# Leaky ReLUs of a graph-attention layer: from VectorE instructions to ScalarE's Prelu

## The chip, the cores and the metric

The kernel runs on one core of one Trainium2 chip. The metric is device time in microseconds (us), here of that one core. Engines are named as the profile names them: PE is TensorE's matmul, PEld its weight load, DVE is VectorE, ACT is ScalarE, POOL is GpSimd, SP is SyncE, whose queue issues nearly all transfers. Each engine works through its own queue in order and waits on semaphores for the others.

## The reference, cut to what matters

There are 128 graphs of 128 nodes with 512 features. Layer 0 is masked multi-head attention with 8 heads, a ReLU, a residual and a layer norm. Layer 1, in which the change lies, is graph attention with one head:

```python
Wh = jnp.matmul(h, W)                      # h is layer 0's output
s_i, s_j = Wh_sg @ a1, Wh_sg @ a2
e = _leaky(s_i[:, :, None] + s_j[:, None, :])      # first leaky ReLU, slope 0.2
e = jnp.where(adj > 0, e, jnp.float32(-9000000000000000.0))
attention = jax.nn.softmax(e, axis=1)
h_prime = jnp.einsum('bij,bjf->bif', attention, Wh)
return _leaky(h_prime)                             # second leaky ReLU
# outside: x = _layernorm(x + layer1(x))
```

So for each of the 128 graphs a leaky ReLU is applied to a 128x128 matrix ahead of the softmax, and another one to the 128x512 product behind it.

## The kernel before, in words

All data is float32. The kernel goes over the graphs in two interleaved streams. The projections of layer 0 (`st_` banks, matmuls of L367) are made for groups of four graphs, the output projection of layer 0 and the projection of layer 1 (banks `p_y`, `p_w`, `p_x`, matmuls of L448) for pairs; each of these products is a seven-product block scheme whose partial results ScalarE copies out of PSUM (L344, L348, L459, L770) and VectorE adds up. Attention of layer 0 is the class `Softmax` (logits L520, exponentials L554, division L568, product L600), its norm is `LayerZero`, and layer 1's projection is `LayerOne`.

The class `Edge` is layer 1 behind its projection, one object for each graph. Its methods, in order:

- `sender` (L798, ScalarE) adds s_i to the mask; the result is transposed, for 117 graphs by a store (L806), a fetch (L812) and a block transposition on VectorE (`turn_blocks`, L817), for the last 11 by TensorE into the PSUM bank `p_e` (`turn`, L802).
- `add` (L820, ScalarE) adds s_j, a value for each partition, to the transposed matrix.
- `maxima` (VectorE) applies the leaky ReLU into the tile `att` (L825) and takes the row maxima of that, negated (L827).
- `exp` (L831, ScalarE) exponentiates and sums; `divide` (VectorE) takes the reciprocal (L835) and scales (L836).
- `product` (L841, TensorE) multiplies by `Wh` into the bank `p_h`.
- `copy` (L847, ScalarE) copies that bank into the tile `z`.
- `residual` (VectorE) applies the second leaky ReLU in place (L851) and adds the residual (L852).
- `stats` (L644 and L646, VectorE), `rstd` (L650 and L652, POOL), `apply` (L665 on VectorE or L661 on ScalarE) and `store` (SP queue, L865) are the layer norm and the output.

The order of all instructions is written out by hand. A loop over steps `t` covers the first 124 graphs, in pairs of steps with one order for even and one for odd `t`; in both `edge.add()` comes directly ahead of the block that holds `edge.maxima()` and `fin.residual()`, where `fin` is the edge one step older. The last graphs are ordered by a string, `PLAN`, which names a job and a method for each piece; `e0` to `e10` are the last eleven edges. In the loop the tile `att` has two buffers and `z` one; in the plan these tiles lie in the space of weights that are no longer needed, which the profile calls `wk` and `wq`.

Two more names occur below: `wv_n` (L408) is a ring of weight blocks fetched from DRAM for the value projection, and `x_dram` (L716) is the store of layer 0's output, fetched back transposed as `xz` (L241).

Of the kernel before, what the change touches and what calls it, by code (L numbers as in the profile page):

```python
# [11 lines left out]
AF = mybir.ActivationFunctionType  # L12
ALU = mybir.AluOpType
# [6 lines left out]
ALPHA = 0.2  # L20
# [4 lines left out]
def kernel(  # L25
# [59 lines left out]
    nc = tc.nc  # L85
    B, P, D = x.shape
# [9 lines left out]
    small = ctx.enter_context(tc.tile_pool(name="small", bufs=3))  # L96
# [136 lines left out]
    X, XT, XS, Q, K, V, MF, OT, X1T, X1, WH = ({} for _ in range(11))  # L233
# [59 lines left out]
    )  # L293

    def strassen(bank, multiply, read, add):


# [17 lines left out]
        def block(h, o, role, name=None):  # L315
            return lambda: add(h, o, p[role], t.get(name))

        return {
            "p1": product("y", 0, True),
            "t0": copy("t0", 0),  # L320
            "p5": product("w", 4, True),
            "p6": product("y", 5),
            "t2": copy("t2", 1),
            "p2": product("x", 1, True),
            "c11": block(0, 0, "x", "t0"),
            "p7": product("y", 6),
            "t3": copy("t3", 1),
            "c22": block(1, 1, "w", "t3"),
            "p4": product("y", 3),
# [20 lines left out]
    def group_product(g, turn, weight, out, transposed_out, bias=None):  # L350
# [30 lines left out]
        def add(h, o, p, t):  # L381
            if t is None:
                copy_out(out(h, o), p, o, bias)
            else:
                nc.vector.tensor_add(out(h, o), p, t)

        return strassen(bank, multiply, read, add)

    def products(g):
# [110 lines left out]
    class Softmax:  # L500
# [28 lines left out]
        def add(self, r):  # L529
            if r == 0:  # L530
                self.pa = self.tile("pa", [P, 4, H, 32])
            by_head = self.pa.rearrange("p b h k -> p h b k")
            mf = MF[self.b].rearrange("p (b k) -> p b k", b=4)
            nc.vector.tensor_add(  # L534
                by_head[:, r * NC : (r + 1) * NC],
                self.lg[r].rearrange("p c (b k) -> p c b k", b=4),
                mf.unsqueeze(1).to_broadcast([P, NC, 4, 32]),
            )
# [8 lines left out]
        def maxima(self):  # L547
            self.add(0)
            self.add(1)
            self.reduce()  # L550
# [58 lines left out]
        def copy(self):  # L609
            pair, h = divmod(self.b, 2)  # L610
            if h == 0:
                OT[pair] = self.tile("oT", [P, NC, 2 * P])
            for c in range(NC):
                nc.scalar.activation(  # L614
                    OT[pair][:, c, h * P : (h + 1) * P],
                    self.oT[:, c, :],
                    AF.Identity,
                    bias=b_cols[:, 1, c : c + 1],
                )
# [49 lines left out]
    class LayerZero:  # L669
# [12 lines left out]
        def residual(self, h, src, o=None):  # L682
            dst = X1[2 * self.pair + h]
            if o is not None:
                dst = dst[:, o * HALF : (o + 1) * HALF]
            nc.vector.scalar_tensor_tensor(dst, src, 0.0, dst, op0=ALU.max, op1=ALU.add)
# [94 lines left out]
    class Edge:  # L781
# [35 lines left out]
            nc.vector.transpose(self.e, self.ez.rearrange("p a e -> p (a e)"))  # L817

        def add(self):
            nc.scalar.activation(self.e, self.p, AF.Identity, bias=self.s[:, 1, :])  # L820

        def maxima(self):
            e = self.e
            self.att = self.tile("att", [P, P], small, 2)
            nc.vector.scalar_tensor_tensor(self.att, e, ALPHA, e, op0=ALU.mult, op1=ALU.max)  # L825
            self.nmax = small.tile([P, 1], F32, name="nmax1", bufs=4)
            nc.vector.tensor_reduce(self.nmax, self.att, AX.X, ALU.max, negate=True)  # L827

# [15 lines left out]

        def copy(self):
            self.z = self.tile("z", [P, D], work, 1)
            nc.scalar.copy(self.z, self.ph)  # L847

        def residual(self):
            z = self.z  # L850
            nc.vector.scalar_tensor_tensor(z, z, ALPHA, z, op0=ALU.mult, op1=ALU.max)  # L851
            nc.vector.tensor_add(z, z, X1.pop(self.b))  # L852

        def stats(self):
            self.norm = Norm(self.z, self.on_scalar)
# [567 lines left out]
```

## Time and profile before

| | |
|---|---|
| three timed runs, us | 2368.99, 2369.56, 2372.61 |
| median, us | 2369.56 |
| span of the profiled execution, us | 2364.5 |
| own device time of the profiled execution | not recorded beside the span; the median of the timed runs is 5.1 us above it |
| granted TensorE clock, mean | 0.998 |
| busy: PE, PEld, DVE, ACT, POOL, us | 2330.4, 1976.3, 1836.7, 1507.4, 769.9 |
| instructions in the span | 43985 |

The span is the time from the first to the last instruction in one profiled execution. A share of busy time is an average over the whole span: the profile has a short start-up, a long even stretch in which the same two steps come again and again, and a drain of some 110 us at the end, and these have to be looked at one by one. A matmul counts as busy from its start to a modelled end, so neighbouring matmuls overlap. An idle gap is shown with the instruction whose end is taken to have released the engine.

### The profile page before, as it was taken

How to read it: one execution, taken by the hardware profiler on the slowest of the kernel's cores; microseconds unless marked ns; L12 is line 12 of the kernel's file. 1: busy time of each engine (PE TensorE's matmuls, PEld its weight loads, DVE VectorE, ACT ScalarE, POOL GpSimd, SP SyncE). 2: the span in 40 equal slices, each digit the busy share in tenths (PEclk: the TensorE clock that was granted, in tenths of full speed). 3: DMA queues.
4: the chain of work that ended last, by engine and by line, in shares of the span. 5: the costliest groups of instructions: out<-in, count | busy, mean ns of one | idle time of the engine just before them, and what ended most of it. 6: DMA issues, size and time to landing. Idle time of an engine off the chain costs nothing.

```text
span 2364.5 us, 43985 instructions
## 1 busy us (share of the span) xinstructions
PE 2330.4 (99%) x13362; PEld 1976.3 (84%) x13362; DVE 1836.7 (78%) x3718; ACT 1507.4 (64%) x5459; POOL 769.9 (33%) x1191
## 2 busy tenths in 40 slices
PE   8999999999999999999999999999999999999997
PEld 7878888888888888888888888888888888888875
DVE  5677787877878877878778778778787787787778
ACT  3656666667666666666576666666665766666675
POOL 2232333323333323333233333233332333332325
PEclk9999999999999999999999999999999999999999
DMA  6655555555555555555555555555555555555453
GB/s 196 189 158 164 169 165 178 163 164 169 173 158 175 166 168 165 168 170 173 163 171 167 163 175 168 168 163 170 172 169 164 170 168 163 176 167 168 152 164 114
DMA packets 435564, 395.31 MB, mean 167 GB/s; under 512 B 108280, under 2 KB 339328, under 8 KB 435328
## 3 DMA queue, kind: packets, MB, share of 16 engines
q1 hardware_dynamic: 435008, 392.23, 54.2%
q8 instruction: 107, 1.75, 0.3%
q14 instruction: 129, 1.06, 0.2%
q10 hardware_dynamic: 320, 0.26, 0.0%
HBM read 248.58 MB, written 143.72 MB: 166 GB/s over the span
## 4 chain that ended last, share of the span: by engine, by line
PE 85%; DVE 5%; DMA 4%; ACT 3%; issue 1%; SPq 1%; POOL 1%; DVEq 0%; POOLq 0%; ACTq 0%
PE st_y L367 25%; PE p_y L448 16%; PE st_w L367 13%; PE p_w L448 8%; PE st_x L367 6%; PE lg L520 5%; PE p_oT L600 4%; PE p_h L841 4%; PE p_x L448 4%; ACT pa L568 1%; DMA paz<-pa_dram 1%; DMA pa_dram<-pa 1%; DVE st L644 1%; DVE pa L534 1%; DVE nmax L543 0%
## 5 line engine op out<-in xcount | busy, mean ns | idle before, releaser
L650 POOL TENSOR_SCALAR ve<-mv 128x1 f32<-128x1 f32 x256 | 69.8, 273 | 1425.4 <-DVE mv L646 1420.0
L554 ACT ACTIVATE pa<-pa,nmax 128x128 f32<-128x128 f32 x1008 | 393.4, 394 | 5.6 <-DVE nmax L543 5.5
L568 ACT ACTIVATE pa<-pa,rs 128x128 f32<-128x128 f32 x1008 | 326.6, 391 | 28.5 <-DVE rs L564 28.5
L344 ACT COPY st_t<-st_y 128x512 f32<-128x512 f32 x192 | 111.0, 578 | 158.9 <-PE st_y L367 83.2
L459 ACT COPY pr_t<-p_y 128x257 f32<-128x257 f32 (+1 forms) x375 | 137.3, 366 | 110.8 <-PE p_y L448 109.9
L348 ACT ACTIVATE st_t<-st_y,b_cols 128x256 f32<-128x256 f32 x192 | 79.9, 467 | 198.9 <-PE st_y L367 198.9
L554 ACT ACTIVATION_READ_ACCUMULATOR pa<-pa,nmax 128x1 f32 x1008 | 192.3, 191 | 0.0
L587 DVE STREAM_TRANSPOSE pa<-paz 128x1024 f32<-128x1024 f32 x126 | 156.9, 1245 | 18.1 <-DMA paz<-pa_dram 15.6
L534 DVE TENSOR_TENSOR pa<-lg,mf 128x512 f32<-128x512 f32 x252 | 161.0, 680 | 0.2 <-PE lg L520 0.2
L614 ACT ACTIVATE oT<-p_oT,b_cols 128x128 f32<-128x128 f32 x504 | 137.1, 381 | 33.8 <-PE p_oT L600 33.6
L543 DVE TENSOR_REDUCE nmax<-pa 128x8 f32<-128x1024 f32 x126 | 151.7, 1204 | 2.2
L652 POOL TENSOR_TENSOR rstd<-ve,mhalf 128x1 f32<-128x1 f32 x256 | 146.2, 571 | 21.3
L600 PEld LDWEIGHTS p_oT<-pa,v 128*64 128x64 f32 x2016 | 108.6, 137 | 49.5 <-issue 23.7
L520 PE MATMUL lg<-kT,qT 64*128 64x128 f32 x2048 | 132.1, 279 | 0.0
L448 PE MATMUL p_y<-wo,oT 128*128 128x256 f32 x504 | 129.6, 380 | 1.7 <-ACT p_y L469 1.7
L448 PE MATMUL p_y<-w,x1T 128*128 128x257 f32 x496 | 128.8, 382 | 1.7 <-ACT wk L459 1.6
L448 PE MATMUL p_y<-wo,oS 128*128 128x256 f32 x504 | 129.5, 379 | 0.5 <-ACT pr_t L459 0.5
L520 PEld LDWEIGHTS lg<-kT,qT 64*128 64x128 f32 x2048 | 119.4, 188 | 12.3 <-issue 11.6
L448 PE MATMUL p_y<-w,x1S 128*128 128x257 f32 x496 | 128.0, 380 | 0.2 <-ACT wk L459 0.2
L600 PE MATMUL p_oT<-pa,v 128*64 128x128 f32 x2016 | 125.0, 276 | 2.3 <-DVE pa L587 1.9
L367 PE MATMUL st_y<-wv_n,xT 128*128 128x256 f32 x512 | 121.3, 380 | 3.3 <-ACT st_t L344 3.3
L367 PE MATMUL st_y<-xT,wk 128*128 128x256 f32 x512 | 124.0, 385 | 0.0
(201 smaller groups left out, 5869.6 us busy)
## 6 DMA issues: line engine op xcount, KB each, us to landing
pa_dram<-pa SPq DMA_DIRECT2D x126, 512.0 KB, 2.9
paz<-pa_dram SPq DMA_DIRECT2D x504, 128.0 KB, 2.8
wv_n<-wv SPq DMA_DIRECT2D x224, 256.0 KB, 3.0
x<-in_x_dram SPq DMA_DIRECT2D x128, 256.0 KB, 2.9
x_dram<-x SPq DMA_DIRECT2D x128, 256.0 KB, 2.3
xz<-x_dram SPq DMA_DIRECT2D x512, 64.0 KB, 2.0
xz<-in_x_dram SPq DMA_DIRECT2D x496, 64.0 KB, 2.3
out_dram<-z SPq DMA_DIRECT2D x120, 256.0 KB, 2.5
```

Source lines behind the costliest of these rows:

```text
L367: nc.tensor.matmul(p[:, m, :], lhs, rhs, start=start and m == 0 and kc == 0, stop=True, skip_group_check=True,)
L448: nc.tensor.matmul(p[:, :width], xs()[n][:, kc, :], w[:, PLACE[n], kc, :], start=start and kc == 0, stop=True, skip_group_check=True,)
L459: nc.scalar.copy(t[:, :width], p[:, :width])
L520: nc.tensor.matmul(self.lg[r][:, c, :], q[rows, c, cols], k[rows, c, cols], start=c == 0, stop=True, skip_group_check=True,)
L534: nc.vector.tensor_add(by_head[:, r * NC : (r + 1) * NC], self.lg[r].rearrange("p c (b k) -> p c b k", b=4), mf.unsqueeze(1).to_broadcast( ...
L543: nc.vector.tensor_reduce(self.nmax, by_head, AX.XY, ALU.max, negate=True)
L554: nc.scalar.activation(self.pa[:, :, h, :], self.pa[:, :, h, :], AF.Exp, bias=self.nmax[:, h : h + 1], accum_out=self.sums[:, h : h + 1],)
L568: nc.scalar.activation(self.pa[:, :, h, :], self.pa[:, :, h, :], AF.Copy, scale=self.rs[:, h : h + 1])
L587: nc.vector.transpose(self.paT.rearrange("p h (a i) -> p a h i", i=32), self.paz.rearrange("p a (h k) -> p a h k", k=32),)
L600: nc.tensor.matmul(self.oT[r * HD : (r + 1) * HD, c, :], v[:, h * HD : (h + 1) * HD], self.paT[:, r * NC + c, :], start=c == 0, stop=True, ...
L614: nc.scalar.activation(OT[pair][:, c, h * P : (h + 1) * P], self.oT[:, c, :], AF.Identity, bias=b_cols[:, 1, c : c + 1],)
L652: nc.gpsimd.tensor_tensor(self.r, ve, mhalf, ALU.pow)
```

## The change

The two leaky ReLUs move from instructions of their own on VectorE into the two ScalarE instructions that come ahead of them. `add` now computes Prelu(p + s_j) with slope 0.2 and writes straight to `att`; `copy` computes Prelu of the PSUM bank. The tile `att` is taken in `add` instead of `maxima`. Nothing else is moved: the loop, the plan and all other instructions stand where they stood, and lines behind L820 are up to two lower or one higher in the file.

```diff
         def add(self):
-            nc.scalar.activation(self.e, self.p, AF.Identity, bias=self.s[:, 1, :])
+            self.att = self.tile("att", [P, P], small, 2)
+            nc.scalar.activation(
+                self.att, self.p, AF.Prelu, bias=self.s[:, 1, :], alpha=ALPHA
+            )
 
         def maxima(self):
-            e = self.e
-            self.att = self.tile("att", [P, P], small, 2)
-            nc.vector.scalar_tensor_tensor(self.att, e, ALPHA, e, op0=ALU.mult, op1=ALU.max)
             self.nmax = small.tile([P, 1], F32, name="nmax1", bufs=4)
             nc.vector.tensor_reduce(self.nmax, self.att, AX.X, ALU.max, negate=True)
...
         def copy(self):
             self.z = self.tile("z", [P, D], work, 1)
-            nc.scalar.copy(self.z, self.ph)
+            nc.scalar.activation(self.z, self.ph, AF.Prelu, alpha=ALPHA)
 
         def residual(self):
-            z = self.z
-            nc.vector.scalar_tensor_tensor(z, z, ALPHA, z, op0=ALU.mult, op1=ALU.max)
-            nc.vector.tensor_add(z, z, X1.pop(self.b))
+            nc.vector.tensor_add(self.z, self.z, X1.pop(self.b))
```

## The prediction

> **What bounds the kernel now.** I read the page's busy times first, then the busy time by stretch, then what TensorE waited for, then VectorE's timeline at the end. The page says that TensorE is all but full:
>
> ```profile
> PE 2330.4 (99%) x13362; PEld 1976.3 (84%) x13362; DVE 1836.7 (78%) x3718; ACT 1507.4 (64%) x5459; POOL 769.9 (33%) x1191
> ```
>
> The table of stretches (start:end and length in us, then busy us of each engine) shows where the 1% is:
>
> ```profile
> 150.00:400.00 250.00, 247.32 (x1431) 210.42 (x1430) 194.43 (x390) 158.62 (x579) 81.29 (x122) 1.00 0.54 166
> 400.00:1000.00 600.00, 599.51 (x3469) 510.74 (x3468) 473.14 (x954) 384.83 (x1398) 194.26 (x300) 1.00 0.55 168
> ...
> 2255.00:2320.00 65.00, 59.95 (x368) 46.57 (x367) 50.39 (x105) 50.15 (x177) 24.76 (x49) 1.00 0.51 163
> 2320.00:2364.00 44.00, 31.06 (x116) 20.09 (x114) 36.12 (x86) 21.07 (x55) 24.32 (x48) 0.91 0.31 106
> ```
>
> From 400 to 1000 us PE is idle for 0.5 us of 600, and the two stretches up to 2255 us look alike (0.3 us each). There VectorE, busy for 79%, is cover only. PE has gaps from 150 to 400 us (2.7 us) and in the drain: 5.1 us from 2255 to 2320, 12.9 us after. No edge work lies before 148 us, where L825 first runs, so the 11.9 idle us before 150 us stay. The change can win about 21 us at the very most. What PE waited for, first from 150 to 2255 us, then from 2255 us on (total, times, longest):
>
> ```profile
> PE st_y L367 <- ACT st_t L344: 1.9, 1, 1.9
> PE st_w L367 <- DVE x1T L246: 0.5, 2, 0.3
> PE p_oT L600 <- DVE pa L587: 0.4, 1, 0.4
> ```
>
> ```profile
> PE p_h L841 <- DVE wk L836: 4.5, 5, 2.6
> PE p_y L448 <- ACT wk L459: 1.7, 3, 0.9
> PE st_y L367 <- DMA wv_n<-wv: 1.7, 1, 1.7
> ```
>
> The largest is the division L836 ahead of an edge product, and on VectorE the removed instructions stand ahead of that division. The last one, 2.6 us at 2349.6 us, leads into the chain that sets the end.
>
> **What the skill says.** (1) The Trainium skill, "ScalarE: Activation LUTs", section *What ACT_TABLE_LOAD costs*, gives one element per cycle for every function: 186 ns + 0.833 ns an element with immediates, 280 ns + 0.833 with one pointer operand. That is 613 ns for a 128x512 activation with immediates and 387 ns for 128x128 with a pointer bias; the trace has 586 ns for the present copy L847 and 406 for L820, within 5%. (2) "ScalarE activation tables: per-element evaluation and per-set limits", section *What a function is on this engine*: with the same operands an activation costs the same whichever table is read, functions in one set need no switch, and a switch is one load of 1283 ns. The trace has a single load, of 1283 ns, at 2.6 us; no run here shows Prelu yet. In the built program of the changed kernel there is again one load, with Exp and Prelu both behind it. (3) "Trainium Kernel Development and Optimization", section *Performance Expectations*, warns that matmul busy time is a poor measure since matmuls overlap. So I checked the pace: in the chain that ended last, four matmuls of 256 columns take 0.86 or 0.87 us everywhere in the even part. Full there does mean full.
>
> **The change part by part.** The rows concerned (count, then total us and mean ns):
>
> ```profile
> L851 DVE SCALAR_TENSOR_TENSOR z<-z 128x512 f32<-128x512 f32 x120 | 81.2, 677 | 0.1
> ...
> L825 DVE SCALAR_TENSOR_TENSOR att<-e_turned 128x128 f32<-128x128 f32 x117 | 42.3, 361 | 0.2 <-ACT e_turned L820 0.2
> ...
> L847 ACT COPY z<-p_h 128x512 f32<-128x512 f32 x120 | 70.3, 586 | 83.5 <-PE p_h L841 74.0 <-DMA out_dram<-z 4.3 <-DMA paz<-pa_dram 4.0
> ...
> L820 ACT ACTIVATE e_turned<-e_turned,wh 128x128 f32<-128x128 f32 x117 | 47.5, 406 | 6.5 <-DVE e_turned L817 6.5
> ...
> L920 ACT ACT_TABLE_LOAD x1 | 1.3, 1283 | 2.6 <-issue 2.6
> ```
>
> *Removed from VectorE:* 128 instructions of L851 (120 x 677 ns and 8 x 672 ns: 86.6 us) and 128 of L825 (117 x 361 and 11 x 376: 46.4 us), 133 us in all.
>
> *On ScalarE:* no instruction more. `add` keeps its operands, so I take 0 for it. `copy` goes from a copy to an activation with immediates. Bounds: nothing below the copy's 586 ns is to be expected since both read and write the same elements, and above, the skill's 613 (+27 ns), or the nearest activation of that size in the trace, with two pointers, 829 ns (L661; +243 ns). I take +0.02 us; 128 x 0.02 = 2.6 us on ScalarE, at most 31. In the even part ScalarE is busy for 23.4 us of the 36.2 us of a pair of graphs, and waits for PE before these very copies (74.0 us at L847), so either bound is hidden there by PE.
>
> *Waits.* `add` now writes `att`. In the built program it waits in the loop for VectorE's transposition alone, so the two buffers of `att` bring no wait for a product; the copies of `p_y` queued behind it are not held up. L827 waits for ScalarE instead of for L825, and `add` stands well ahead of it. PE, POOL and the SP queue keep their order, and no transfer is added. With orders fixed and hardly any duration longer, things can only come earlier, apart from contention.
>
> *What is gained, 150 to 2255 us.* The 1.9 us gap at 174 us: TensorE waits for st_t on ScalarE, that is queued behind L568, which waits for the reciprocal L564, and in front of this VectorE works without a break from 165.3 us, an L825 (0.3) and an L851 (0.7) among it. Gain 1.0. The 0.4 us at 379 us (L587, behind a fetch whose chain has an L851 and an L825): gain 0.4. What is late elsewhere is PE itself: 133 us of VectorE's work end in idle time. Sum 1.4; bounds 0 and 2.3.
>
> *Drain up to 2349.6 us.* The 1.7 us for wv_n at 2271.5 us follow from a chain of L851 (0.6 at 2261.0), norm, store x_dram, and its fetch in the SP queue ahead of the wv_n fetch: gain 0.7. Four of the five waits for L836 sum to 4.5 - 2.6 = 1.9 us, with an L825 ahead of each and an L851 ahead of most: gain 1.4. The waits for L459 (1.7) are partly behind an exponential that waits for L827: gain 0.4. The wait for rt L835 (0.4): 0.2. What is late next is ScalarE, without a break from 2275.6 to 2286.7 us, and PE. Sum 2.7; bounds 1 and 5.
>
> *The last chain*, from the timeline of VectorE (start, duration):
>
> ```profile
> 2349.41 0.69 DVE L851 SCALAR_TENSOR_TENSOR wq<-wq 128x512 f32<-128x512 f32 x1 [0.70 <-ACT wq L847]
> 2350.14 0.69 DVE L852 TENSOR_TENSOR wq<-wq,x 128x512 f32<-128x512 f32 x1
> 2350.75 0.28 DVE L825 SCALAR_TENSOR_TENSOR wk<-wk 128x128 f32<-128x128 f32 x1
> 2351.07 0.29 DVE L827 TENSOR_REDUCE nmax<-wk 128x1 f32<-128x128 f32 x1
> ...
> 2352.45 0.28 DVE L825 SCALAR_TENSOR_TENSOR wk<-wk 128x128 f32<-128x128 f32 x1
> ...
> 2357.32 0.66 DVE L851 SCALAR_TENSOR_TENSOR wq<-wq 128x512 f32<-128x512 f32 x1
> 2358.01 0.69 DVE L852 TENSOR_TENSOR wq<-wq,x 128x512 f32<-128x512 f32 x1
> 2358.74 0.69 DVE L644 BATCH_NORM_STATS2 st<-wq 128x6 f32<-128x512 f32 x1
> ```
>
> Without L851 the addition starts at 2349.41, the maxima at 2350.14 (`add` on ScalarE ends at 2349.65), instead of 2351.07: -0.93. The second L825, 0.32 with its gap, goes too: the division of the last edge ends 1.25 earlier, and so do its product and its copy, which ended at 2357.07 and would end at 2355.82. From that copy to the end of the statistics were 2.57 us (2359.64); without L851, and with the statistics of the edge before finished by 2355.7, they are 0.03 + 0.73 + 0.89 = 1.65: -0.92. Sum 2.2; 0.06 for longer copies is within rounding; with the upper bound on the copies some 0.5 less.
>
> Total: 1.4 + 2.7 + 2.2 = 6.3 us. The span goes from 2364.5 to 2358.2; with the 5.1 us by which the median stands above the span, 2369.6 goes to **2363.3**.
>
> **The rivals.** (a) *PE takes the gaps back*: another input is late next at each gap, and only the last chain's 2.2 us stay: 2367.4, no change that can be told. For it: the chain that ended last names ScalarE and DMA in the drain as well. Against it: VectorE heads PE's waits there. (b) *Slower: activation tables reload* between Exp and Prelu, on ScalarE, 1283 ns a switch (the row above). Of the eleven last edges each would switch up to four times: 44 x 1.283 = 56 us, where ScalarE is idle for 65 - 50.2 + 44 - 21.1 = 37.8 us from 2255 us on; 18 us over, so 2369.6 - 6.3 + 18 = 2381 and more if the even part (10.3 of 12.8 idle us a pair) breaks too. It decides from some five switches in the last chain, which eat the 6.3 us. Against it: one load in the built program. (c) *Prelu is simply dearer* than a copy. With the upper bound, three on the last path cost 0.7 us: 2364. It would need over 2 us each to lose.
>
> **How the numbers follow.** Told apart from no change is about 0.2%, 4.7 us. The forecast has 0.69: it ranges over the bounds 0 to 2.3, 1 to 5 and 1.5 to 2.5, so 2.5 to 9.8 us, of which I put 0.05 under 4.7 us. Rival (a) has 0.23, (c) counts inside these two, (b) and unseen contention 0.08, of which 0.02 end within 0.2%. Faster 0.64, same 0.30, slower 0.06. The range reaches from 2369.6 - 9.8, and 1 us for the scatter of the runs (3.6 us between the three shown), 2359, to 2368, past rival (a).
>
> **What would show it.** Right: L851 and L825 gone, DVE near 1704 us, ACT within 10 us of 1507, one table load, PE's busy time unchanged, the gap at 174 us near 0.9, PE's waits for L836 nearly halved, and the last statistics some 2 us nearer to the last copy's start. Wrong: more table loads, Prelu rows over 0.7 us, or gaps of the same length with other releasers.

## The result and the profile after

| | before | after |
|---|---|---|
| timed runs, us | 2368.99 to 2372.61 (4) | 2350.80 to 2352.52 (4) |
| median, us | 2369.89 | 2351.74 |
| ratio, 95% interval | | 0.9927 [0.9914, 0.9940] |
| span of the profiled execution, us | 2364.5 | 2350.7 |
| device time of that execution, us | not recorded | 2352.52 |

The change wins 18.1 us, three times the 6.3 forecast, and 2351.7 lies below the range. In the page's line of busy times only VectorE moved by much, by 129.8 us; ScalarE did not:

```profile
PE 2324.7 (99%) x13362; PEld 1978.8 (84%) x13362; DVE 1706.9 (73%) x3462; ACT 1506.7 (64%) x5459; POOL 763.0 (32%) x1191
```

The groups of instructions of the kernel after (count, total us, mean ns, idle time before, and its releasers) show what the new ScalarE instructions cost, 599 and 406 ns, and that there is one table load:

```profile
L847 ACT ACTIVATE z<-p_h 128x512 f32<-128x512 f32 x120 | 71.9, 599 | 78.0 <-PE p_h L841 55.0 <-DMA paz<-pa_dram 22.0 <-DMA out_dram<-z 0.4
...
L821 ACT ACTIVATE att<-e_turned,wh 128x128 f32<-128x128 f32 x117 | 47.5, 406 | 2.5 <-DVE e_turned L817 2.4
...
L918 ACT ACT_TABLE_LOAD x1 | 1.3, 1283 | 2.6 <-issue 2.6
```

The table of stretches of the kernel after (start:end, length, busy us of PE, PEld, DVE, ACT, POOL, then the clock's share). The last two stretches are those of before from 2255 us on, counted back from the end:

```profile
150.00:400.00 250.00, 249.89 (x1445) 213.29 (x1444) 183.31 (x371) 160.62 (x587) 81.88 (x124) 1.00 0.55 168
400.00:1000.00 600.00, 600.00 (x3479) 513.36 (x3478) 441.00 (x890) 386.19 (x1405) 194.99 (x302) 1.00 0.55 168
2241.20:2306.20 65.00, 61.65 (x382) 49.40 (x381) 45.88 (x96) 49.22 (x183) 22.52 (x40) 1.00 0.51 162
2306.20:2350.70 44.50, 34.86 (x139) 24.39 (x137) 34.04 (x82) 25.85 (x62) 26.71 (x62) 0.97 0.38 128
```

From 400 to 1000 us PE's busy time grew by 0.5 us, but there are 10 matmuls more in the same 600 us (3479 against 3469). That is the gain which idle time doesn't show: ten matmuls at a pace of 0.216 us, that of the 256-column ones, are about 2.2 us. In the drain, PE did 382 + 139 = 521 matmuls in its last 109.5 us, where before did 368 + 116 = 484 in 109.

**Where the time came from.** Both traces hold the same 13362 matmuls in the same order. The table gives the time between the same two of them, in us; the columns' heads are the times in the profile of before. The first column counts from the first matmul (1.3 us after the span's start), and the last from the last `p_w` matmul at 2349.6 us, so it has the last wait and the last edge products in it. "Again" and "third" are further profiles of the same two programs (from the experiments).

| | start to 165 | 165 to 400 | to 1000 | to 1600 | to 2241 | to 2320 | to 2350 | to the end |
|---|---|---|---|---|---|---|---|---|
| before | 163.9 | 235.14 | 599.86 | 599.82 | 641.09 | 78.99 | 29.48 | 14.88 |
| before, again | 164.4 | 234.43 | 598.63 | 600.29 | 641.34 | 84.05 | 29.49 | 14.20 |
| before, third | 166.0 | 239.92 | 601.79 | 600.64 | 641.13 | 81.97 | 29.51 | 14.22 |
| after | 166.1 | 231.67 | 597.89 | 598.48 | 639.84 | 77.21 | 26.53 | 11.70 |
| after, again | 163.1 | 233.48 | 597.71 | 598.41 | 639.84 | 80.22 | 26.55 | 11.69 |

(The start is free of the change: it varies mostly in one stretch, 60 to 95 us, ahead of all edge work, that takes 34.1 to 38.4 us over all programs profiled, and 34.1 and 37.9 us in the two profiles of after.) The even part from 165 to 2241 us gives 3.46 + 1.96 + 1.34 + 1.25 = 8.0 us, the drain up to 2349.6 us 1.8 + 2.95 = 4.7, the last chain 3.2, and the start takes 2.2: 13.7 us of span. The rest of the 18.1 lies between the profiled executions and the medians. Around the span are 2352.52 - 2350.7 = 1.8 us (1.7 to 1.9 in nearly every run); with these the profiled execution of before took 2366.3 us, 3.6 below its median, and that of after 0.8 above its own. The profile of before is of a short execution. The profiles "again" are of longer ones (2369.99 and 2354.18 us): there the even part gives 5.2, the drain 6.8, the last chain 2.5 and the start 1.4, 15.9 in all. So the split of the gain by stretches depends on which executions were profiled; the third profile of before has an even part of 2083.5 us, where the other two have 2075.9 and 2074.7.

**The waits.** In the even part of after no idle gap of PE is left to list. The waits of PE's weight loads (total, times, longest) had shown more than PE's own gaps. Before, from 150 to 2255 us, without the rows that both kernels have alike:

```profile
PEld st_w L367 <- DVE x1T L246: 3.3, 6, 0.7
PEld st_y L367 <- ACT st_t L344: 2.3, 1, 2.3
PEld p_y L448 <- ACT pr_t L459: 2.1, 5, 0.6
PEld p_w L448 <- issue: 1.6, 4, 0.5
PEld p_oT L600 <- DVE pa L587: 0.9, 2, 0.7
PEld st_w L367 <- issue: 0.9, 3, 0.3
```

In the two rows with "issue" the profile finds no releaser. The same view of after, from 150 to 2241 us, all that is left beside the common rows:

```profile
PEld st_y L367 <- ACT st_t L344: 0.5, 1, 0.5
PEld p_oT L600 <- DVE pa L587: 0.2, 1, 0.2
PEld st_w L367 <- issue: 0.2, 1, 0.2
```

These six rows of before sum to 11.1 us, 8.6 of them with a releaser named; 0.9 are left after. The Trainium skill, "Perfetto Trace Analysis", section *Identifying the Most-Contended Engine*, says that matmul busy time doesn't tell how near to its limit TensorE is, since its instructions are pipelined, and names the share of peak arithmetic and the busy share of the weight loads as the measures. On busy time the case agrees (the share of the weight loads, 84% before and after, tells little here; their waits do): a matmul of 256 columns is shown for some 380 ns and the next starts 216 ns later, so one that comes up to 160 ns late leaves no gap at all.

One late engine, VectorE, can be followed behind most of these rows. ScalarE's wait for VectorE's reciprocal, in the row of the softmax division, first in before and then in after:

```profile
L568 ACT ACTIVATE pa<-pa,rs 128x128 f32<-128x128 f32 x1008 | 326.6, 391 | 28.5 <-DVE rs L564 28.5
```

```profile
L568 ACT ACTIVATE pa<-pa,rs 128x128 f32<-128x128 f32 x1008 | 327.6, 397 | 0.7 <-DVE rs L564 0.6
```

**How VectorE's lateness gets into a prefetch.** One of the nine places where `st_w` came late, in the timeline of before (start, duration, engine):

```profile
826.86 1.55 DVE L665 TENSOR_SCALAR z<-z,mv,rstd 128x512 f32<-128x512 f32 x1
...
828.43 0.34 SPq L865 DMA_DIRECT2D out_dram<-z  x1
...
828.86 0.39 SPq L806 DMA_DIRECT2D e_dram<-e  x1
...
829.34 0.40 SPq L408 DMA_DIRECT2D wv_n<-wv  x1
...
831.19 1.29 DVE L246 STREAM_TRANSPOSE x1T<-xz 128x512 f32<-128x512 f32 x2
...
832.62 1.75 PE L367 MATMUL st_w<-wv_n,xT 128*128 128x256 f32 x7 [0.30 <-DVE x1T L246]
```

The same place after:

```profile
823.17 1.54 DVE L665 TENSOR_SCALAR z<-z,mv,rstd 128x512 f32<-128x512 f32 x1
...
824.74 0.34 SPq L863 DMA_DIRECT2D out_dram<-z  x1
...
825.17 0.39 SPq L806 DMA_DIRECT2D e_dram<-e  x1
...
825.65 0.41 SPq L408 DMA_DIRECT2D wv_n<-wv  x1
...
828.54 1.29 DVE L246 STREAM_TRANSPOSE x1T<-xz 128x512 f32<-128x512 f32 x2
...
829.73 1.46 PE L367 MATMUL st_w<-wv_n,xT 128*128 128x256 f32 x6
```

The store of `z` waits for the norm L665 on VectorE, and the SP queue works in order, so the fetch of `wv_n` behind the store waits too. It takes 3.1 us to land: in before at 829.34 + 3.14 = 832.48 us, and the matmul starts at 832.62. The profile puts this wait down to the transposition `x1T` of VectorE, which ends at 832.48 too. But the matmul doesn't read `x1T`, and in after it starts at 829.73, while that transposition still runs, to 829.83. After, the norm starts 6.6 us ahead of the matmul instead of 5.8, and the fetch goes out 4.1 us ahead of it instead of 3.3, so it lands about 1 us before it is needed.

In the drain PE's waits of after, from 2241 us on, are these (before: 4.5 for L836, 1.7 for L459 and 1.7 for `wv_n`):

```profile
PE p_h L841 <- DVE wk L836: 1.9, 2, 1.5
PE p_y L448 <- ACT wk L459: 1.3, 2, 0.9
PE st_y L367 <- DMA wv_n<-wv: 1.1, 1, 1.1
```

### The profile page after: what moved, and what is told of

It reads as the page before. It is cut to its first block, busy times and chain, and to the rows that moved or that the text cites. A ratio compares the mean times of both kernels' runs of the same rounds, so it can differ in the third digit from the quotient of the medians.

```text
span 2350.7 us, 43613 instructions
## 1 busy us (share of the span) xinstructions
PE 2324.7 (99%) x13362; PEld 1978.8 (84%) x13362; DVE 1706.9 (73%) x3462; ACT 1506.7 (64%) x5459; POOL 763.0 (32%) x1191
## 4 chain that ended last, share of the span: by engine, by line
PE 92%; DMA 3%; DVE 2%; ACT 1%; SPq 1%; issue 1%; POOL 0%; POOLq 0%; DVEq 0%; ACTq 0%
PE st_y L367 26%; PE p_y L448 18%; PE st_w L367 13%; PE p_w L448 9%; PE st_x L367 7%; PE lg L520 5%; PE p_oT L600 5%; PE p_h L841 4%; PE p_x L448 4%; DMA paz<-pa_dram 1%; DMA pa_dram<-pa 1%; ACT pa L568 0%; ACT pa L554 0%; SPq L581 0%; DMA e_dram<-e 0%
## 5 line engine op out<-in xcount | busy, mean ns | idle before, releaser
L459 ACT COPY pr_t<-p_y 128x257 f32<-128x257 f32 (+1 forms) x375 | 139.0, 371 | 125.1 <-PE p_y L448 120.7
L587 DVE STREAM_TRANSPOSE pa<-paz 128x1024 f32<-128x1024 f32 x126 | 156.9, 1246 | 15.7 <-DMA paz<-pa_dram 14.1
```

The costliest lines, as they stand in the source:

```text
L459: nc.scalar.copy(t[:, :width], p[:, :width])
L587: nc.vector.transpose(self.paT.rearrange("p h (a i) -> p a h i", i=32), self.paz.rearrange("p a (h k) -> p a h k", k=32),)
```

## The experiments

Three accounts of the excess were set against each other. *Occupancy*: VectorE does too much in a pair of steps, and taking 122 us out of the loop lets it run ahead wherever that work stands. *Chain*: only what stands directly ahead of the maxima and the norm matters. *Store*: the work matters since it delays the store of `z` that the fetch of `wv_n` is queued behind. "Even part" is the time from the matmul at 165 us to that at 2241 us, against 2075.9 us in the first profile of before. In the texts of what was expected, theory Q is occupancy and S the store; C puts the waits down to VectorE's and ScalarE's own lateness without the store, and E holds that the even part is covered by TensorE and the gain comes from the last edges. Each group of runs has its own runs of before: median 2372.56, 2373.46 and 2371.18 us.

### The loop alone and the plan alone

`loop_only` makes both edits for the 117 edges of the loop, `plan_only` for the eleven of the plan; VectorE's two instructions are left out for the same edges (not in the cut):

```diff
+            if not self.homes:        # loop_only; plan_only: if self.homes:
+                self.att = self.tile("att", [P, P], small, 2)
+                nc.scalar.activation(
+                    self.att, self.p, AF.Prelu, bias=self.s[:, 1, :], alpha=ALPHA
+                )
+                return
             nc.scalar.activation(self.e, self.p, AF.Identity, bias=self.s[:, 1, :])
...
+            if not self.homes:        # plan_only: if self.homes:
+                nc.scalar.activation(self.z, self.ph, AF.Prelu, alpha=ALPHA)
+            else:
+                nc.scalar.copy(self.z, self.ph)
```

> Both Prelus for the 117 edges of the loop alone; the eleven edges of the plan keep VectorE's leaky ReLUs. Theory Q (VectorE's queue): in the even part the removed instructions had stood ahead of what TensorE waits for, in many waits too short to be shown as idle time; of the 16 us by which TensorE came earlier after 165 us in the changed kernel 8.0 lie before 2241 us, so this kernel should win about 8 us (6 to 11) and its drain should be as long as in the kernel before. Theory E (end chain): the even part is covered by TensorE and the gain comes from the last edges; this kernel should win at most 2 us.

> Both Prelus for the last eleven edges alone. Theory Q: only the drain gains, 4.8 us of waits up to the last products and 3.2 behind them, so 8 us (6 to 10), and the waits in the even part stay as in the kernel before (weight loads of st_w waiting some 3 us in all). Theory E: nearly the whole 18 us.

`loop_only`: 2361.34 us, 0.9956 [0.9938, 0.9973]. Its even part is 8.3 us shorter, stretch by stretch as in after; from 2241 us to the end it gains 0.4. `plan_only`: 2365.70 us, 0.9975 [0.9963, 0.9986]; its even part is 1.2 us longer than before's, and from 2241 us on it gains 1.1, 2.9 and 3.2, as after does. So the two parts are separate and, within intervals of some 3 to 4 us each way, add up: 11.2 + 6.9 = 18.1 us. The weight loads of `plan_only` wait as before in the even part:

```profile
PEld st_w L367 <- DVE x1T L246: 4.4, 9, 0.8
PEld p_oT L600 <- DVE pa L587: 2.7, 6, 0.9
```

### One leaky ReLU each

```diff
 # z_only: L825 stays, L851 goes
-            nc.scalar.copy(self.z, self.ph)
+            nc.scalar.activation(self.z, self.ph, AF.Prelu, alpha=ALPHA)
 # att_only: L851 stays, L825 goes
-            nc.scalar.activation(self.e, self.p, AF.Identity, bias=self.s[:, 1, :])
+            nc.scalar.activation(
+                self.att, self.p, AF.Prelu, bias=self.s[:, 1, :], alpha=ALPHA
+            )
```

> Only the second leaky ReLU (128x512, 677 ns on VectorE) is moved into the copy. Theory Q: gain in proportion to VectorE's removed time, 86.6 of 133 us, so about 12 us of 18 (9 to 14). Theory E: the two on the last chain count 0.73 and 0.92, the rest of the drain about half, so about 5 us.

> Only the first leaky ReLU (128x128, 361 ns) is moved into the addition of s_j. Theory Q: 46.4 of 133 us, so about 6 us of 18 (4 to 9); both parts together should about add up to the whole. Theory E: about 3 us. If instead one part alone wins nearly the whole, a threshold at one wait decides and not the sum of the time.

`z_only`: 2358.12 us, 0.9935 [0.9918, 0.9953], a gain of 14.4. `att_only`: 2361.44 us, 0.9956 [0.9941, 0.9971], a gain of 11.1. They sum to 25.6 where both together give 18.1, and both are above what had been expected of them (9 to 14 and 4 to 9 us in proportion to VectorE's time, 5 and 3 by the end of the kernel alone). In the even part each alone gives most of it, 6.9 and 6.3 us of 8.0. The stretches say why: several kernels end on the same 597.71, 598.41 and 639.84 us from 400 to 2241 us (`att_only` the first two, `z_only` the last two, `loop_only`, `no_leaky` and `after_again` all three). That is taken for TensorE's own time, with nothing waited for: no kernel is below it. To take away 46 us of VectorE's work or 87 us of it leads to this floor in two of three stretches.

### The store behind the fetch

`before_order` is the kernel before with one call moved: the loop issues the store of `z` behind `e_dram` and the fetch of `wv_n` (the call stood once in the order for even and once in that for odd steps; the cut shows one). `after_order` has the same move made in the kernel after.

```diff
                 fin.apply()
-                fin.store()
...
             group()
+            fin.store()
```

> The kernel before, with the loop's store of the result z issued on the SP queue after the fetch of wv_n and the store of e that used to stand behind it; VectorE's work is the one of before. Theory S (SP queue): in the even part most of the lost time comes from wv_n landing late, since its fetch stands behind a store that waits for VectorE's norm; this order alone should win the wv_n part of the ledger, about 3 us of the profile's 8, and more where the runs of before scatter upward. Theory C (compute waits): the waits are for VectorE's additions and for ScalarE's copies behind the reciprocals, so the order changes less than 1 us.

> The changed kernel with the same order of the store. Its even part has no waits left by the profile, so both theories expect no change against the changed kernel (2350 to 2354). If it is faster, waits too short to be seen were still there; if slower, the late store of z holds up the next copy into z.

`before_order`: 2367.15 us, 0.9975 [0.9964, 0.9986]: 6.3 us by the medians (some 3 to 9 with the interval), a third of the gain, with none of VectorE's work taken away. In the profile the even part is 3.5 us shorter, and 3.0 of that are the late starts of `st_w`: all nine are gone, as the store account had said (about 3). Its timeline at the place shown above:

```profile
825.83 1.54 DVE L665 TENSOR_SCALAR z<-z,mv,rstd 128x512 f32<-128x512 f32 x1
...
826.35 0.32 SPq L806 DMA_DIRECT2D e_dram<-e  x1
...
826.76 0.38 SPq L408 DMA_DIRECT2D wv_n<-wv  x1
...
827.39 0.34 SPq L865 DMA_DIRECT2D out_dram<-z  x1
...
831.11 1.89 PE L367 MATMUL st_w<-wv_n,xT 128*128 128x256 f32 x8
```

The fetch goes out before the norm ends and 4.4 us ahead of its matmul. The row `st_w <- DVE x1T` is gone from the waits of weight loads, though the transposition `x1T` is still there: it was not a wait for `x1T`. Of what stays, the largest rows with a releaser are VectorE's work itself and ScalarE's copies:

```profile
PEld p_oT L600 <- DVE pa L587: 1.7, 6, 0.5
PEld st_y L367 <- ACT st_t L344: 1.5, 1, 1.5
```

`after_order`: 2355.50 us, 0.9923 [0.9904, 0.9942], in its bounds the same as after, and its even part is 0.3 us longer. With the VectorE instructions gone, the order of the store brings nothing more.

### VectorE's work put back in another place

`filler_late` is the kernel after with instructions of the removed sizes put back behind the statistics, where no maximum and no residual has their result as an input. They change no value. The norm's application and the store of `z` do stand behind them.

```diff
             self.norm.stats()
+            if not self.homes:
+                for part in (self.z, self.z[:, :P]):
+                    nc.vector.scalar_tensor_tensor(part, part, 1.0, part, op0=ALU.mult, op1=ALU.max)
```

> The changed kernel with two VectorE instructions of the removed kind and sizes put back in each loop edge, without effect on the values, directly behind the statistics: VectorE is as busy as before, the chain from s_j to the exponential and from the product to the statistics stays short. If occupancy of VectorE's queue is what counts, the even part loses again nearly what loop_only won, 8 to 11 us against the changed kernel; if it is the shorter edge chain, it stays within 2 us of the changed kernel.

2358.17 us, 0.9936 [0.9920, 0.9953]. Both accounts missed: the even part is 3.5 us longer than that of after, where 8 to 11 were expected if VectorE's total decides and under 2 if only the chain does. This does not settle how much each counts. By busy time VectorE got back only 80.5 us (1787.5 against 1706.9), not the 122 of the loop. 1.7 of the 3.5 us are one late fetch of `wv_n` at 618 us, of a kind that `after_again` has too, and 0.9 the gap behind ScalarE near 180 us. ScalarE's wait for the reciprocal L564 is 13.2 us, between the 28.5 of before and the 0.6 of after, so the amount of VectorE's work does count also where no edge's maximum depends on it; the share that goes to its place stays open.

### Twice the work

`before_plus` goes the other way: each removed instruction stands twice in the loop of the kernel before, the second with slope 1.0, which changes no value.

```diff
             nc.vector.scalar_tensor_tensor(self.att, e, ALPHA, e, op0=ALU.mult, op1=ALU.max)
+            if not self.homes:
+                nc.vector.scalar_tensor_tensor(
+                    self.att, self.att, 1.0, self.att, op0=ALU.mult, op1=ALU.max
+                )
...
             nc.vector.scalar_tensor_tensor(z, z, ALPHA, z, op0=ALU.mult, op1=ALU.max)
+            if not self.homes:
+                nc.vector.scalar_tensor_tensor(z, z, 1.0, z, op0=ALU.mult, op1=ALU.max)
```

> The kernel before with a second VectorE instruction of each removed kind and size behind the first, in the loop's 117 edges, without effect on the values: 122 us more on VectorE, whose busy share would be 83%. If the even part of the kernel before was covered by TensorE and its waits a fixed remainder, nothing changes beyond 1 us. If VectorE's queue is at the edge, so that each pair of steps loses time as its work grows, it loses more than the loop's 122 us had cost (10 to 11 us by loop_only): 15 to 60 us.

2460.89 us, 1.0359 [1.0336, 1.0381]: 89.7 us more for 122.8 us of VectorE's work, 0.73 us for each; the even part of its profile is 87.2 us longer. The instructions stand on the chain of an edge, so amount and place are raised together here. VectorE is only 81% busy in the even part, PE 97%:

```profile
400.00:1000.00 600.00, 584.20 (x3293) 486.48 (x3293) 486.97 (x980) 372.99 (x1356) 185.02 (x283) 1.00 0.53 161
```

PE waits for ScalarE's copies of `p_y`, nearly once in each pair of graphs (57.8 of the 87.2 us are lost ahead of products of `p_y`), and ScalarE waits for VectorE. PE's waits in this kernel from 150 to 2241 us, and then ScalarE's:

```profile
PE p_y L448 <- ACT pr_t L459: 34.3, 54, 1.5
```

```profile
ACT pa L568 <- DVE rs L564: 95.2, 56, 2.3
```

Over the whole kernel, ScalarE's 28.5 us of waiting for that reciprocal in before are 100.3 here and 0.6 in after. The kernel before stood at a knee: 122 us of VectorE less win some 11 us, 122 more cost 90. An engine at 79% was at the edge of what its dependencies allow.

### Does Prelu itself cost anything?

`no_leaky` leaves out the two leaky ReLUs: Identity and a copy stand in place of Prelu.

```diff
-                self.att, self.p, AF.Prelu, bias=self.s[:, 1, :], alpha=ALPHA
+                self.att, self.p, AF.Identity, bias=self.s[:, 1, :]
...
-            nc.scalar.activation(self.z, self.ph, AF.Prelu, alpha=ALPHA)
+            nc.scalar.copy(self.z, self.ph)
```

> The changed kernel with Identity and a copy in place of the two Prelus: both leaky ReLUs of layer 1 are left out. If Prelu costs what copy and Identity cost, the time is that of the changed kernel within 1 us and the rows L821 and L847 keep their means within 30 ns; if Prelu is dearer, it is faster by what the last chain has of it, three times the difference or more.

2353.19 us, 0.9921 [0.9903, 0.9938], no different from after within the interval (4 us each way). Its group of copies:

```profile
L847 ACT COPY z<-p_h 128x512 f32<-128x512 f32 x120 | 70.5, 588 | 77.6 <-PE p_h L841 46.8 <-DMA paz<-pa_dram 30.0 <-DMA out_dram<-z 0.4
```

588 ns against 599 with Prelu, and 412 against 406 for `add`: 11 ns dearer and 6 ns cheaper, so at most 1.4 us of ScalarE's 1507 for all 128 copies.

### The same programs again

`before_again` and `before_third` are the kernel before, `after_again` the kernel after, unchanged, to see what one profile is worth.

> The kernel before, unchanged, for a second profile. If the first profile was an ordinary run, span and ledger agree with it within 1 us; if it was one of the short runs among those of 2365 to 2381 us, the span is 2367 to 2376 us and the difference lies in the waits of the even part (theory Q) or in the start (nothing to do with the change).

> As before_again, a third profile of the same program, to see which stretches of it scatter from run to run.

> The changed kernel, unchanged, for a second profile on the chip of the others: its even part (165 to 2241 us on the scale of before) should repeat within 0.5 us if it has no waits left, and only start and drain scatter.

2369.99, 2378.34 and 2354.18 us; their stretches are in the table of the result. Two expectations missed. `before_again` differs from the first profile by 5.1 us in the drain, not in the even part, which is 1.2 us shorter. The even part of `after_again` is 1.6 us longer than that of after, not within 0.5: one fetch of `wv_n` came 1.6 us late at 395.7 us, so the kernel after is not free of such waits. `before_third` shows what lengthens an execution of before. PE's waits from 150 to 2241 us have a row that is 0.3 us in the first profile:

```profile
PE st_w L367 <- DMA wv_n<-wv: 4.1, 3, 2.3
```

The longest, 2.3 us, ends at 403.9 us, and behind it the stretches show the granted clock (the share ahead of the last two columns) fall:

```profile
398.00:402.00 4.00, 3.59 (x16) 2.53 (x14) 3.59 (x7) 3.71 (x17) 2.08 (x2) 1.00 0.72 252
402.00:410.00 8.00, 6.08 (x19) 4.42 (x20) 0.97 (x3) 1.89 (x7) 0.00 (x0) 0.79 0.45 124
```

0.79 over 8 us is 3.4 us at half clock, a further 1.7 us of TensorE's work. The Trainium skill, "TensorE: Matmul & The Clock Gate", section *Part 1: The HAM clock gate*, says that the clock is full or half and is set anew in windows of 3.4 us by how busy TensorE was, and half after an idle window. Here the 3.4 us and the half clock agree, but no idle window of that length was needed: a pause of 2.3 us came ahead of it. Nor does the length of a pause alone decide: a pause of 1.94 us, ending at 178.7 us in `before_third`, was followed by half clock from 179.8 us, and the same pause of 1.94 us at 176.6 us in the first profile of before, and one of 2.47 us at 96.1 us in after, were not. What decides is open here. `before_third` has three such windows ahead of its last chain, `before_again` two in a row in the drain, `after_again` one, after none. Over the runs of before in the experiments the mean clock goes with the time: 14 runs at 0.998 have a mean of 2368.6 us, 26 at 0.997 of 2373.4, ten at 0.996 of 2376.5; the four of after have 0.998 and 0.999. That late inputs, fetches of `wv_n` most of all, bring these windows is what the traces show side by side. It was not tried by itself.

## Why the prediction was wrong

The forecast was 6.3 us and the gain 18.1. The 11.8 us between them are, by the first profiles: 6.6 in the even part, 2.0 in the drain, 1.0 in the last chain and 4.4 in the step from the span to the median, less 2.2 that the start took at random.

**"With orders fixed ... things can only come earlier", no dearer ScalarE: right.** VectorE fell to 1706.9 us (1704 forecast), ScalarE is at 1506.7 (within 10 of 1507), there is one table load, and the copy costs 13 ns more where 20 were taken and the nearer bound, an estimate, was 27. Rivals (b) and (c) are out: there is no reload, and `no_leaky` puts the price of Prelu at nothing that shows in the time.

**"What is gained, 150 to 2255 us: sum 1.4; bounds 0 and 2.3": wrong, the step that failed.** It measured 8.0 in the first profiles, 5.2 between the typical ones, and 11.2 by the medians of `loop_only`. The sum was bounded by PE's idle gaps ("Full there does mean full"), and these were 3.8 us in all, less than what was won. The check of the pace looked at four matmuls in the chain that ended last, which said nothing on how many groups in 2100 us start late. Taken from one matmul to the next in both profiles, the 8.0 us are: the gap at 174 us, 1.8 (1.0 forecast); products behind L587, 0.8 (0.4 forecast); and three kinds that were given nothing: nine late starts of `st_w` behind a fetch of `wv_n`, 2.9, products of `p_y` behind ScalarE's copies, 1.5, and those of `p_w` behind an addition of VectorE, 1.0. "What is late elsewhere is PE itself: 133 us of VectorE's work end in idle time" was the sentence to doubt: ScalarE's 28.5 us of waiting for VectorE's reciprocal stood in the page of before. They show a VectorE that others wait for, though it is idle for a fifth of the time.

**"VectorE ... is cover only", at 79%: wrong.** `before_plus` shows the knee. That VectorE's work isn't spread evenly over a pair of graphs, so that what it does next is often awaited, is the likely reason; the waits fit it, but no run spreads the same work out.

**"PE, POOL and the SP queue keep their order": right, and the reason for a gain that was overlooked.** A fixed order with a store ahead of a fetch hands VectorE's lateness on. The forecast used that for the one gap of 1.7 us in the drain, behind another store (`x_dram`), and not for the loop, where the fetch stands behind the store of `z`. `before_order` puts it at 6.3 us by the medians and 3.0 in the profile.

**"Drain: sum 2.7; bounds 1 and 5": mechanism right, too small.** 4.7 us in the first profiles, inside the bounds, and 6.8 between those "again", outside; the waits for L836 went from 4.5 to 1.9 us as said. The part from 2320 to 2349.6 us is firm, 2.9 to 3.0 between any two profiles of before and after; the part before it holds the wait for `wv_n`, which was 1.7, 4.0 and 3.2 us in the three profiles of before, and 1.1 and 2.6 in those of after.

**"The last chain: sum 2.2": right.** 3.2 in the first profiles, of which 0.7 is the clock: the chain of before is 14.88 us long there and 14.20 in both others, and its last products ran in a half-clock window. Against these it is 2.5. After, the timeline of VectorE has the addition 0.13 us behind the copy's end, and then the statistics:

```profile
2343.48 0.69 DVE L644 BATCH_NORM_STATS2 st<-wq 128x6 f32<-128x512 f32 x1
2344.21 0.18 DVE L646 BATCH_NORM_AGGREGATE mv<-st 128x2 f32<-128x6 f32 x1
2344.31 0.66 DVE L850 TENSOR_TENSOR wq<-wq,x 128x512 f32<-128x512 f32 x1
2345.01 0.69 DVE L644 BATCH_NORM_STATS2 st<-wq 128x6 f32<-128x512 f32 x1
2345.74 0.18 DVE L646 BATCH_NORM_AGGREGATE mv<-st 128x2 f32<-128x6 f32 x1
```

The last copy runs from 2343.58 to 2344.18 us and the statistics end at 2345.92: 1.74 us where 1.65 were forecast and 2.57 had been.

**"5.1 us by which the median stands above the span": wrong.** It was carried over to the kernel after as if it were fixed. Around a span are 1.8 us; the other 3.3 are how much shorter the profiled execution of before was than a middle one. The two later profiles show what such executions have more: late fetches and half-clock windows. The execution of after lies 0.8 us above its median, so the median falls by 18.1 - 13.7 = 4.4 us more than the profiles. How much of this the change itself takes away, and how much is the luck of which execution was profiled, one profile each can't tell.

Rival (a), that PE takes the gaps back, is out: the even part and the drain gain beside the last chain, and from 400 to 2241 us the stretches of after stand within 0.2 us of TensorE's floor.

## What to carry to other kernels

A TensorE that is 99% busy may still have several us to win: before bounding a gain by its idle gaps, read what its weight loads wait for, and how long the co-engines wait for each other; afterwards, compare the time between the same two matmuls, since busy time hides a late start. Look in each in-order DMA queue for a store ahead of a prefetch; the prefetch is as late as the engine that the store waits for. Moving the store has a price of its own, small here: in `before_order` ScalarE's copies into `z` wait 18.1 us for the store where they waited 4.3. A releaser that the profile names may only have ended at the same moment; look whether the instruction reads it. One profile is one execution: add what lies around its span, see where it stands among the timed runs, and take waits that differ from run to run as part of what a change may remove.

## What the runs showed of the hardware

Prelu on ScalarE with an immediate slope costs nearly what the copy or the biased Identity costs that it replaces, 599 ns against 586 and 406 against 406, and the program has one table load for Exp and Prelu together. A pause of TensorE of 2.3 us was followed by 3.4 us at half clock, and other pauses of 1.9 to 2.5 us were not. A VectorE that is busy for 81% of the time can be what holds TensorE: in `before_plus` each further us on it cost 0.73.
